# A decoder layer on one core: the place of the cross-attention's output product among the transposes of its step

## The chip, the cores and the metric

The kernel runs on one core of a Trainium2 chip. The metric is the device time of one execution, in microseconds (us). The kernel before took 2285.08 us, the median of three runs (2284.96 to 2286.03).

A core has five engines, each with an instruction queue of its own: TensorE (PE in the profile; its weight loads are shown apart, as PEld), VectorE (DVE), ScalarE (ACT), GpSimd (POOL) and SyncE (SP), which issues most of the transfers. Matrix products go into PSUM, which the kernel uses as eight banks of 128 x 512 floats; everything else lies in SBUF.

## What is computed

One decoder layer with the normalisation behind each block, for 32 sequences of 256 tokens and 256 features:

```
x = layernorm(x + self_attention(x))            # 16 query heads of 64, 4 key heads, rotary, alibi
x = layernorm(x + cross_attention(x, ctx, ctx)) # 16 heads of 16, windows of 64, rotary, mask by cell
x = layernorm(x + feed_forward(x))              # 8-bit activations, ternary weights, 1024 inner
```

The part that the change touches is the end of the cross-attention. Its heads' outputs `o` of one token are normalised, projected, and added to the residual; then the sum is normalised:

```
y = _ln(o, ln_o_w, ln_o_b) @ w_o.T + b_o
x = layernorm(x + y)
```

In the kernel the scale `ln_o_w` is multiplied into the weights beforehand, and bias terms are already in the residual.

## The kernel before

A batch is one sequence: two tiles of 128 tokens (t = 0 and 1). The program is written out as slots, two to a step (part 0 and part 1), eight steps to a batch. In every step one eighth of a batch's self-attention runs: transposes `t` of the last step's probabilities (`self_turn`, L447), scores `s` for this step (`self_scores`, L394), and in every second step the values `o` (L464) and the spread of the inverse sums `R` (L479). A second pipeline runs nine steps behind with the cross-attention: scores `xs` (L656), exponentials (L686), transposes `xt` (`cross_turn`, L695), values `xo` (`cross_values`, L711), and transposes back `xr` (`cross_back`, L731). Everything else is written as generators that do a piece of work at each slot: the projections of the next batch (`self_inputs`, L331), the self-attention's output (`self_output`, L495), the context's keys and values (`cross_inputs`), the cross-attention's output (`cross_output`) and the feed-forward (`feed_forward`, L798 and L845). A number that a generator yields is the number of slots until its next piece; nothing means one.

TensorE, VectorE and ScalarE run their instructions exactly in the order in which the program issues them (`manual_schedule`). The order on GpSimd and SyncE is set by the framework. So the order of the calls within a slot decides what waits behind what. In a slot the generators that are due run first. Then in part 0 come the self-attention's transposes, `cross_back` and `cross_turn`, then the deferred ScalarE scalings in `last` (`flush`), and then the scores. In part 1 come `cross_values` and the normalisation of the self-attention's output (`self_normal`, L487). What is left in `last` is issued at the end of each slot.

`cross_output(b, t)` starts 29 + 8t slots after its batch. Its pieces are:

- the statistics of the heads' output `on` (VectorE) and their reciprocal deviation `rstd` (three GpSimd instructions, `rstd_of`, L185 to L187);
- one slot on, the scaling of `on` on ScalarE, put into `last` (`scaled`, L199);
- one slot on, `transposed`: two transposes `zoT` on TensorE (L205) and a copy into `zT` on ScalarE (L206);
- one slot on, in part 0, the product `xw` = zT x weights (L757), the sum with the residual into `x2` (VectorE, L761), its statistics and its `rstd`;
- one slot on, the scaling of `x2` on ScalarE, put into `last`.

The product's slot is part 0 of a step: of step 16 after the batch's start for the first tile, of step 20 for the second. Generators come first, so on TensorE `xw` stands ahead of that step's transposes `t`, `xr` and `xt`. `feed_forward(b)` begins with the maximum of both tiles of `x2` (VectorE) in step 21.

In the names of the profile, `zT` is the transposed normalised output, `xw` the PSUM bank of the product, `xoT` the copy of the values that `xr` transposes, `pT` and `xpT` the copies of the transposed probabilities of the two attentions.

Of the kernel before, what the change touches and what calls it, by code (L numbers as in the profile page):

```python
# [13 lines left out]
ALU = mybir.AluOpType  # L14
# [5 lines left out]
D = 256  # L20
NDC = D // P
# [29 lines left out]
def kernel(  # L51
# [27 lines left out]
    nc = tc.nc  # L79
# [5 lines left out]
    def ctile(shape, dtype, name):  # L85
        return const.tile(shape, dtype, name=name, tag=name)
# [3 lines left out]
    def bank(name, shape=(P, 512), dtype=F32):  # L90
        return ps.tile(list(shape), dtype, tag="b", name=name)
# [12 lines left out]
    def work(name, shape, bufs=2, dtype=F32):  # L104
        return sb.tile(list(shape), dtype, tag=name, name=name, bufs=bufs)

    def small(name, n):
        return sb.tile([P, 8], F32, tag="small", name=name, bufs=48)[:, 0:n]
# [31 lines left out]
    xo_w = ctile([P, NDC, D], F32, "xo_w")  # L140
# [15 lines left out]
    for i in range(2):  # L156


        t = ctile([P, (NT + 1) * XH * XE + 32 - XE], F32, f"xvaug{i}")
# [14 lines left out]
    def stats(src, name):  # L174

        st = small("st", 6)
        mv = small(f"mv_{name}", 2)
        nc.vector.bn_stats(st, src)
        nc.vector.bn_aggr(mv, st)
        return mv  # L180

    def rstd_of(mv, name):

        rb = small(f"rstd_{name}", 2)
        nc.gpsimd.tensor_scalar(rb[:, 0:1], mv[:, 1:2], EPS, None, ALU.add)  # L185
        nc.gpsimd.tensor_tensor(rb[:, 0:1], rb[:, 0:1], neg_half[:, 0:1], ALU.pow)
        nc.gpsimd.tensor_scalar(rb[:, 1:2], mv[:, 0:1], rb[:, 0:1], -1.0, ALU.mult, ALU.mult)  # L187
        return rb


    last = []

    def flush():
        while last:
            last.pop(0)()
# [5 lines left out]
    def transposed(dst, src, name):  # L201

        pt = bank(name)
        for dc in range(NDC):
            nc.tensor.transpose(pt[:, dc * P : (dc + 1) * P], src[:, dc * P : (dc + 1) * P], ident)  # L205
        nc.scalar.copy(dst, pt[:, 0 : NDC * P].rearrange("p (c t) -> p c t", t=P))  # L206
# [537 lines left out]
    def cross_output(b, t):  # L744
        s = state[b]
        on = s["on", t]
        mv = stats(on, "zo")
        rstd = rstd_of(mv, "zo")
        yield
        last.append(partial(scaled, on, on, rstd))  # L750
        yield
        zoT = work("zT", [P, NDC, P])
        transposed(zoT, on, "zoT")
        yield
        py = bank("xw")
        for dc in range(NDC):
            nc.tensor.matmul(py[:, 0:D], zoT[:, dc, :], xo_w[:, dc, :], start=(dc == 0), stop=(dc == NDC - 1))  # L757
        if t == 0:
            s["x2"] = work("x2", [P, NT, D])
        h = s["x2"][:, t, :]  # L760
        nc.vector.tensor_tensor(h, py[:, 0:D], s["x1", t], ALU.add)  # L761
        mv = stats(h, "x2")
        rstd = rstd_of(mv, "x2")
        yield
        last.append(partial(scaled, h, h, rstd))


    def feed_forward(b):
# [102 lines left out]
    for b in range(B):  # L871
        s0 = 16 * b
        if b:
            at(s0 - 16, self_inputs(b))
        at(s0 + 2, cross_inputs(b))
        for t in range(NT):
            at(s0 + 2 * (5 + 4 * t), self_output(b, t))
            at(s0 + 2 * (CROSS + 5 + 4 * t) + 1, cross_output(b, t))
        at(s0 + 2 * (CROSS + 11) + 2, feed_forward(b))

    with tc.manual_schedule(engines={mybir.EngineType.PE, mybir.EngineType.DVE, mybir.EngineType.Activation}):
        running = []
        slot = min(starts)
        while starts or running:
            step, part = divmod(slot, 2)
            k, odd = divmod(step - CROSS, 2)
            for gen in starts.pop(slot, ()):
                running.append([slot, gen])

            def cross(f, unit, *more):  # L890
                if 0 <= unit < 4 * B:
                    f(*divmod(unit, 4), *more)

            def own(f, unit):
                if 0 <= unit < 8 * B:
                    f(*divmod(unit, 8))


            def pair(f):
                if step % 2 == 0 and 0 <= step // 2 - 1 < 4 * B:  # L900
                    f(*divmod(step // 2 - 1, 4))

            if part == 0:
                pair(self_inverse)
            else:
                pair(self_spread)
            if part == 1 and not odd:
                cross(cross_exp, k, 0)
            if part == 0 and odd:
                cross(cross_exp, k, 1)  # L910
            for r in list(running):
                if r[0] == slot:
                    wait = next(r[1], r)
                    if wait is r:
                        running.remove(r)
                    else:
                        r[0] += wait or 1
            if part == 0:
                own(self_turn, step - 1)
                if odd:  # L920
                    cross(cross_back, k - 1)
                    cross(cross_turn, k, 0)
                else:
                    cross(cross_turn, k - 1, 1)
                flush()
                own(self_scores, step)
                if not odd:
                    cross(cross_scores, k)
                pair(self_values)
            else:  # L930
                if not odd:
                    cross(cross_values, k - 1)
                pair(self_normal)
            flush()
            slot += 1

# [88 lines left out]
```

## Time and profile before

| | |
|---|---|
| median of 3 runs | 2285.08 us |
| profiled execution | 2288.16 us |
| its span, first to last instruction | 2286.3 us |
| mean granted TensorE clock | 0.985 |
| xw on TensorE (L757): records, mean | 256, 417 ns |
| copy into zT on ScalarE (L206): instances, median | 64, 358 ns |

The durations of the prediction come from the profiled execution. Its span is the time between its first and last instruction. A line of a list of waits names the engine and the line of the waiting instruction, then whom it waited for, and then the total in us, the number of times and the longest. The lines of a timeline have start and duration in us, the engine, the line, the operation, the output and the inputs, how many instructions are merged, and in brackets how long the engine was idle before and what ended it. `PEld` lines are weight loads. A product of 32-bit floats shows as two loads and two matmul records.

In the steady part of the run a batch takes 68.23 us: the first tile's product starts at 1101.92, 1170.16 and 1238.39 us, and the second tile's at 1134.79, 1203.02 and 1271.26.

### The profile page before, as it was taken

The numbers are of one execution on the slowest core, as the hardware profiler recorded it, in microseconds if no ns is written. First come the engines' busy times: TensorE is split into PE (matmuls) and PEld (weight loads), VectorE is DVE, ScalarE is ACT, GpSimd is POOL, SyncE is SP. The second block draws the span as 40 slices with busy tenths as digits, with TensorE's granted clock in tenths as the row PEclk, the third lists the DMA queues.
The fourth block names the chain that finished last, engine by engine and source line by source line (L and its number), as shares of the span: only waits on it lengthen the run. The fifth ranks groups of instructions, "written<-read, shape, count | busy, mean of one in ns | idle before, by whom it ended". The sixth has DMA issues, their size and how long they took to land.

```text
span 2286.3 us, 55642 instructions
## 1 busy us (share of the span) xinstructions
PE 2186.2 (96%) x17828; PEld 1653.7 (72%) x17828; DVE 1709.6 (75%) x6949; ACT 1692.1 (74%) x4961; POOL 1117.3 (49%) x1851
## 2 busy tenths in 40 slices
PE   7999999999999999999999999999999999999983
PEld 5677777777777777777777777777777777777651
DVE  3767777877777777777777777787777787777675
ACT  2677777878777878777878777778777777777762
POOL 5344555554555444545554545454545454545432
PEclk9999999999999999999999999999999999999986
DMA  6312222222222222222222222222222222222111
GB/s 215 89 52 55 65 67 59 58 58 59 66 66 59 59 58 63 64 64 60 60 58 67 57 64 63 60 57 68 55 65 62 62 54 68 59 57 56 31 31 31
DMA packets 191427, 144.09 MB, mean 63 GB/s; under 512 B 107808, under 2 KB 160928, under 8 KB 191136
## 3 DMA queue, kind: packets, MB, share of 16 engines
q1 hardware_dynamic: 189440, 136.95, 24.3%
q8 instruction: 144, 2.36, 0.4%
q10 hardware_dynamic: 1696, 3.57, 0.4%
q14 instruction: 147, 1.20, 0.2%
HBM read 39.50 MB, written 8.39 MB: 21 GB/s over the span
## 4 chain that ended last, share of the span: by engine, by line
PE 71%; DVE 12%; ACT 11%; DMA 2%; issue 2%; POOL 1%; SPq 0%; ACTq 0%; POOLq 0%; DVEq 0%
PE s L394 10%; PE proj L331 10%; PE wo L495 9%; PE t L447 8%; PE o L464 8%; ACT p L420 4%; DVE p L410 4%; PE xt L695 4%; DVE gu L813 3%; PE xw L757 3%; ACT xp L686 3%; PE xv L616 3%; PE ffo L845 2%; PE R L479 2%; PE xk L604 2%; PE v L363 2%
## 5 line engine op out<-in xcount | busy, mean ns | idle before, releaser
L420 ACT ACTIVATE p<-p,nm 128x256 f32<-128x256 f32 x1024 | 507.9, 498 | 156.1 <-DVE nm L410 152.3
L410 DVE CUSTOM_DVE_ANT_0 p<-s,alibi 128x256 f32<-128x256 f32 x1024 | 372.3, 420 | 167.8 <-PE s L394 167.8
L452 ACT COPY pT<-t 128x512 f32<-128x512 f32 x512 | 274.8, 590 | 190.7 <-PE t L447 190.1
L686 ACT ACTIVATE xp<-xp,xnm 128x128 f32<-128x128 f32 x1024 | 326.0, 394 | 4.3 <-DVE xnm L670 4.3
L394 PE MATMUL s<-kT,qT 64*128 64x256 f32 x2048 | 290.9, 403 | 0.0
L447 PE MATMUL t<-ident,p 128*128 128x128 f32 x2048 | 269.2, 274 | 3.2 <-ACT p L420 3.2
L447 PEld LDWEIGHTS t<-ident,p 128*128 128x128 f32 x2048 | 240.4, 141 | 34.8 <-ACT p L420 6.6
L464 PE MATMUL o<-pT,v 128*64 128x256 f32 x2048 | 249.3, 385 | 0.0
L331 PE MATMUL proj<-xT,wq_sb 128*128 128x256 f32 x1024 | 249.1, 387 | 0.0
L495 PE MATMUL wo<-wo_sb,oT 128*128 128x256 f32 x1024 | 245.3, 382 | 0.0
L355 POOL TENSOR_TENSOR qT<-qT,other 128x512 f32<-128x512 f32 x128 | 163.7, 1279 | 152.0 <-DMA other<-psin 83.7
L670 DVE CUSTOM_DVE_ANT_0 xp<-xs,mask 128x128 f32<-128x128 f32 x1024 | 225.7, 286 | 0.9 <-PE xs L656 0.9
L394 PEld LDWEIGHTS s<-kT,qT 64*128 64x128 f32 x2048 | 176.6, 186 | 54.7 <-issue 32.8
L495 PEld LDWEIGHTS wo<-wo_sb,oT 128*128 128x128 f32 x1024 | 189.4, 190 | 33.8 <-issue 10.6
L331 PEld LDWEIGHTS proj<-xT,wq_sb 128*128 128x128 f32 x1024 | 185.6, 191 | 32.7 <-DVE xnm L670 5.9
L464 PEld LDWEIGHTS o<-pT,v 128*64 128x64 f32 x2048 | 136.0, 136 | 97.4 <-issue 41.1
L420 ACT ACTIVATION_READ_ACCUMULATOR p<-p,nm 128x1 f32 x1024 | 192.4, 188 | 0.0
L340 DVE TENSOR_TENSOR psin<-proj,rs_sb 128x512 f32<-128x512 f32 x160 | 110.2, 689 | 96.7 <-PE proj L331 96.5
L697 ACT COPY xpT<-xt 128x512 f32<-128x512 f32 x256 | 153.6, 600 | 8.3 <-PE xt L695 6.6
L695 PE MATMUL xt<-ident,xp 128*128 128x128 f32 x1024 | 155.1, 275 | 0.0
L566 POOL TENSOR_TENSOR qb<-qb,rx_sb 128x256 f32<-128x256 f32 (+1 forms) x96 | 87.7, 913 | 128.9 <-ACT xp L686 76.6
L813 DVE SCALAR_TENSOR_TENSOR gu<-gu,ff 128x512 f32<-128x512 f32 x128 | 82.1, 681 | 74.6 <-ACT gu L812 74.6
(150 smaller groups left out, 4365.0 us busy)
## 6 DMA issues: line engine op xcount, KB each, us to landing
other<-psin SPq DMA_DIRECT2D x640, 64.0 KB, 2.0
xT<-in_xt_dram SPq DMA_DIRECT2D x32, 256.0 KB, 2.9
xs<-in_x_dram SPq DMA_DIRECT2D x32, 256.0 KB, 3.1
cs<-in_ctx_dram SPq DMA_DIRECT2D x32, 256.0 KB, 2.7
other<-qb SPq DMA_DIRECT2D x64, 128.0 KB, 2.0
kTz<-tr SPq DMA_DIRECT2D x256, 32.0 KB, 2.0
other<-qb SPq DMA_DIRECT2D x128, 64.0 KB, 1.9
out_dram<-x SPq DMA_DIRECT2D x32, 256.0 KB, 2.3
```

What stands on the lines that cost most here:

```text
L331: nc.tensor.matmul(pq[:, c * L : (c + 1) * L], w[:, dc, c * P : (c + 1) * P], xT[:, dc, :], start=(dc == 0), stop=(dc == NDC - 1),)
L355: nc.gpsimd.tensor_tensor(d2, d2, other, ALU.add)
L394: nc.tensor.matmul(banks[half][:, rr * L : (rr + 1) * L], qT[rows_, rr, qc * P : (qc + 1) * P], kT[rows_, kc, :], start=(rr == 0), stop=(r ...
L410: nc.vector.tensor_tensor_reduce(p[:, cols], banks[half][:, cols], alibi[:, 2 * (4 * kc + 2 * rp + rr) + half, :], -0.125, 3.0e38, ALU.add ...
L420: nc.scalar.activation(p[:, cols], p[:, cols], AF.Exp, bias=nm[:, rr : rr + 1], scale=-1.0, accum_out=s["sums", i // 2][:, (2 * rp + rr) * ...
L447: nc.tensor.transpose(pt[:, j * P : (j + 1) * P], p[half][:, rr * L + kk * P : rr * L + (kk + 1) * P], ident,)
L452: nc.scalar.copy(pT[half], pt)
L464: nc.tensor.matmul(po[half * HD : (half + 1) * HD, rp * L : (rp + 1) * L], s["v"][:, kk, (2 * kc + half) * HD : (2 * kc + half + 1) * HD], ...
L495: nc.tensor.matmul(py[:, 0:D], s["oT", qc, kc][:, r, :], wo_sb[:, 4 * kc + r, :], start=(kc == 0 and r == 0), stop=(kc == 1 and r == 3),)
L670: nc.vector.tensor_tensor_reduce(p[:, cols], banks[2 * half + j // 2][:, j % 2 * P : (j % 2 + 1) * P], s["mask"][:, qc, :], -1.0, 3.0e38, ...
L686: nc.scalar.activation(p[:, cols], p[:, cols], AF.Exp, bias=s["xnm", i][half][:, j : j + 1], scale=-1.0)
L695: nc.tensor.transpose(pt[:, j * P : (j + 1) * P], p[:, j * P : (j + 1) * P], ident)
```

## The change

The work of the product is put into a function and handed to a new list, `late`. The first tile's generator yields one slot more ahead of it. `late` is emptied at two places of a slot: in part 0 behind `cross_back` and `cross_turn` and ahead of `flush` and the scores, and in part 1 at the end, behind `self_normal`. So the first tile's product, its sum and its statistics are issued at the end of part 1 of step 16 instead of at the beginning of its part 0, and its `x2` is scaled in part 0 of step 17 instead of at the end of part 1 of step 16. The second tile's product is issued in the same slot as before, behind that step's transposes and ahead of its scores, and its `x2` is scaled in the same place as before.

```diff
+    late = []
...
         transposed(zoT, on, "zoT")
-        yield
-        py = bank("xw")
-        for dc in range(NDC):
-            nc.tensor.matmul(py[:, 0:D], zoT[:, dc, :], xo_w[:, dc, :], start=(dc == 0), stop=(dc == NDC - 1))
+        yield 1 + (t == 0)
         if t == 0:
             s["x2"] = work("x2", [P, NT, D])
         h = s["x2"][:, t, :]
-        nc.vector.tensor_tensor(h, py[:, 0:D], s["x1", t], ALU.add)
-        mv = stats(h, "x2")
-        rstd = rstd_of(mv, "x2")
-        yield
-        last.append(partial(scaled, h, h, rstd))
+        more = {}
+
+        def product():
+            py = bank("xw")
+            for dc in range(NDC):
+                nc.tensor.matmul(
+                    py[:, 0:D], zoT[:, dc, :], xo_w[:, dc, :], start=(dc == 0), stop=(dc == NDC - 1)
+                )
+            nc.vector.tensor_tensor(h, py[:, 0:D], s["x1", t], ALU.add)
+            mv = stats(h, "x2")
+            more["rstd"] = rstd_of(mv, "x2")
+
+        late.append(product)
+        yield
+        last.append(partial(scaled, h, h, more["rstd"]))
...
                 else:
                     cross(cross_turn, k - 1, 1)
+                while late:
+                    late.pop(0)()
                 flush()
                 own(self_scores, step)
...
                 pair(self_normal)
+                while late:
+                    late.pop(0)()
             flush()
```

The order of instructions that results, on each engine that it touches (before, then after):

```
first tile
  TensorE  xw t xr xt s o R wo                     t xr xt s o R xw wo
  VectorE  add+stats xrinv on p.. oT hib           xrinv on p.. oT add+stats hib
  ScalarE  oT x2 pT pT xpT p..                     oT pT pT xpT x2 p..
  GpSimd   rstd qb other xqT gu gu                 qb other xqT gu rstd gu
second tile
  TensorE  xw t xr xt s                            t xr xt xw s
  VectorE  add+stats xrinv on p..                  xrinv on add+stats p..
  ScalarE  as before
  GpSimd   as before
```

The order of SyncE's transfers is the same in both kernels.

## The prediction

> **What bounds the kernel now.** First the busy shares of the page, to see which engine can set the end:
>
> ```profile
> PE 2186.2 (96%) x17828; PEld 1653.7 (72%) x17828; DVE 1709.6 (75%) x6949; ACT 1692.1 (74%) x4961; POOL 1117.3 (49%) x1851
> ```
>
> TensorE is busy 96% of the span; no other engine passes 75%. So time can be won only where TensorE stands still, and the second view is the list of who waited for whom (total us, times, longest us):
>
> ```profile
> PE xw L757 <- ACT zT L206: 34.0, 63, 2.9
> PE ffo L845 <- DMA hiT<-hib: 16.6, 4, 9.1
> PE ff L798 <- DMA xiT<-xib: 9.4, 2, 8.4
> ...
> PEld xw L757 <- ACT zT L206: 61.6, 63, 3.2
> ...
> ACT pT L452 <- PE t L447: 190.1, 161, 3.3
> ```
>
> The output product xw is the only place where TensorE waits in every batch: 63 of its 64 instances. All its other waits come 1 to 10 times. ScalarE in turn waits 190.1 us for TensorE's transposes, so elsewhere it is TensorE that is waited for. Third, the chain of waits around batch 15 (start, us, what), to see how the wait sits in the path that sets the end:
>
> ```profile
> 1168.67 0.68 ACT xp L686 x2
> 1169.35 0.50 ACT qb L550 x2
> 1169.85 0.26 ACT zT L206
> 1170.12 0.04 issue
> 1170.16 1.13 PE xw L757 x4
> 1171.29 0.87 PE t L447 x8
> ```
>
> From this xw the chain stays on TensorE to the scores at 1197.32. Then it leaves for VectorE's and ScalarE's softmax, and it comes back through zT into the second tile's xw at 1203.02. So the zT copy, queued behind exponentials and the query bias on ScalarE, is what holds TensorE. Fourth, the timeline of weight loads and of ScalarE there; it has the distances I use (start, us, engine, line):
>
> ```profile
> 1168.39 0.55 PEld L798 LDWEIGHTS <-xiT 128*128 128x128 bf16 x4
> 1170.16 0.73 PEld L757 LDWEIGHTS xw<-xo_w,zT 128*128 128x128 f32 x4 [1.23 <-ACT zT L206]
> 1170.91 1.01 PEld L447 LDWEIGHTS t<-ident,p 128*128 128x128 f32 x8
> 1171.89 0.25 PEld L731 LDWEIGHTS xr<-ident,xoT 128*128 128x128 f32 x2
> ```
>
> ```profile
> 1169.76 0.35 ACT L206 COPY zT<-zoT 128x256 f32<-128x256 f32 x1
> 1170.01 0.37 ACT L720 COPY xoT<-xo 128x256 f32<-128x256 f32 x1
> 1170.27 1.28 ACT L686 ACTIVATE xp<-xp,xnm 128x128 f32<-128x128 f32 x4
> 1171.82 1.07 ACT L452 COPY pT<-t 128x512 f32<-128x512 f32 x2 [0.26 <-PE t L447]
> ```
>
> The picture repeats with the period of a batch (first tile's xw at 1170.16 and 1238.39, 68.23 us apart). In the timeline the load sits idle 1.23 us before nearly every first-tile product and 0.58 to 0.60 us before nearly every second-tile one. 31 and 29 instances have this pattern or a longer wait; the last batches differ.
>
> **The Trainium skill.** "TensorE: Matmul & The Clock Gate", section "Step-by-step: what each phase is for", says that matmuls stay in program order and only weight loads are pulled ahead. The trace agrees: zT is the operand that is loaded, the load itself waits (61.6 us), and nothing behind it runs. "PSUM — Partial Sum Buffer", section "Engine vs sequencer instructions", says that the queues of ScalarE, VectorE and GpSimd are strictly first in, first out; here zT goes at 1169.76, right after the bias at 1169.26, although its transposes were loaded at 1167.38. "Perfetto Trace Analysis", section "Identifying the Most-Contended Engine", warns that matmul busy time overstates TensorE. The load row, 72%, leaves more room, but the chain, 71% on TensorE, says that it is the bound all the same.
>
> **The change part by part.** No arithmetic, transfer or buffer is added or removed, and SP's queue keeps its order. Three moves per batch count.
>
> First tile. On TensorE xw leaves its place ahead of the eight transposes t and goes one slot on, behind R and ahead of wo. The group t can be loaded 0.76 us after the feed-forward load (same pair at 1161.61 and 1162.37), at 1169.15; xr 0.98 us later (1170.91 to 1171.89), at 1170.13. But xr loads xoT, the copy right behind zT, which ends at 1170.38; a load follows its copy by 0.05 (zT ended 1170.11, load 1170.16), so xr goes at 1170.43, after a new wait of 0.30. It went at 1171.89: 1.46 us sooner. Later xw costs its four passes; eight such passes of wo take 1.62 (1176.08 to 1177.70), so 0.81. Net 0.65 us.
>
> Second tile. xw goes behind t, xr, xt and ahead of the scores s. The projection loaded at 1200.84 takes 1.62, t follows at 1202.46, xr at 1203.44 (xoT ended 1203.24: no wait), xt 0.21 later, xw 0.47 after that at 1204.12, s 0.81 + 0.17 later at 1205.10. It was loaded at 1205.61: 0.51 us sooner. Then o, 1.06 after s, at 1206.16. Its fourth matmul, about 0.56 in (6 of 16 loads that take 1.49), needs the second pT copy, which ended at 1206.85, and ScalarE cannot be sooner: it works without a gap from 1196.54. So up to 0.18 of the 0.51 is lost again. I take 0.42, between 0.33 and 0.51.
>
> VectorE moves with it: add, statistics and aggregate, 0.42 + 0.43 + 0.18, about 1.0 us. For the first tile they land behind the oT product and ahead of hib of the feed-forward, where VectorE had idled 0.54 for GpSimd's gu; hib has 5 us of slack, as its transposed copy lands 3.1 us after an issue at 1184.80 and is used at 1193.14. For the second tile they stand ahead of the score reductions; the add can start at 1205.3, VectorE is free again at about 1206.4, and the scores are there 1.17 us after their load (1205.61 to 1206.78), at 1206.27. That costs 0.1 us at most, hidden because ScalarE is busy until 1207.31. Without that cover it would be 0.1 x 29 = 3 us.
>
> ScalarE and GpSimd. The first tile's scaling of x2 (0.60 us) now stands in the next step, between the xpT copy and the exponentials, and waits there for GpSimd's rstd, whose three operations (0.23 + 0.57 + 0.27, about 1.25 with gaps) stand after the first of two gu operations of 1.12. VectorE's statistics end at about 1177.5, gu at about 1178.1, so rstd is done at about 1179.4 and xpT at about 1179.5: no wait. ScalarE there had 1.36 us idle ahead of the exponentials. Second tile: its rstd stays behind the same rotations (begun at 1207.68), its scaling stays at 1210.28.
>
> Sum: 31 x 0.65 + 29 x 0.42 = 20.2 + 12.2 = 32.4 us. The profiled execution took 2288.16 us (span 2286.3); less 32.4 that is 2255.8. The median of the runs is 3.1 lower, 2285.08, so I expect 2253.
>
> **The rivals.** More is won: neither xr nor o waits, because ScalarE runs a little ahead of the trace. For it: both remainders, 0.30 and 0.18, are small. Against: ScalarE's queue has no gap there. 31 x 0.95 + 29 x 0.51 = 44.2, that is 2241.
>
> Less is won: at the second tile the wait only moves, to o (for pT) or to xk (for zcT, whose copies ended 0.6 us ahead of the load at 1211.00), and the first tile keeps half. For it: the unbroken ScalarE queue from 1196.54 to 1210.9. Against: the margins worked out above. 31 x 0.33 = 10, that is 2275.
>
> Slower: ScalarE stands in the first tile's x2 scaling. If GpSimd gets to rstd only behind the second gu, which ended at 1182.20, rstd is done at 1183.5; the exponentials start at 1184.1 instead of 1181.53, and the next xoT copy, which ended at 1185.04 with its load at 1186.13, comes 2.6 later: TensorE loses 2.6 - 1.1 = 1.5 us in a batch. 31 x 1.5 = 46 against 32 won: 2299. It decides once rstd ends later than about 1181.9. Against it: in the order of instructions rstd stands ahead of the second gu, and its inputs (1177.5) are there 4 us before that point. The waits show ScalarE stopped by rstd_x only 5.6 us in all.
>
> No change: zT's wait is replaced in full by xoT's and pT's, 2285. The distances speak against it.
>
> **How the numbers follow.** Forecast 0.64 (2244 to 2264: first tile 0.5 to 0.8, second 0.2 to 0.51), more 0.14, less 0.13, no change 0.03, slower 0.06. The range 2239 to 2273 takes in most of "more" and the nearer part of "less". A difference below 0.2% cannot be told from none in this kernel. Faster 0.91, same 0.03, slower 0.06.
>
> **What would show it.** In the profile after, the wait of xw for zT is gone at both tiles. A wait of xr for xoT of about 0.3 us stands at the first tile only, and perhaps one of o for pT at the second. The distance from one batch's first xw to the next is about 67.2 us. If instead ScalarE's L199 waits for rstd_x in every batch, or TensorE waits for p at t, the rival that ends slower is at work. A distance of 66.8 means that xr did not wait.

## The result, and the profile after

The changed kernel took 2258.61 us, the median of four runs (2256.52 to 2261.18), beside 2285.43 for four runs of the kernel before: a ratio of 0.9883, with a 95% interval of 0.9866 to 0.9900. It is 27 us faster; 32 were expected. The profiled execution took 2257.97 us, with a span of 2256.0.

First the page of the changed kernel: the busy shares, and the chain that ended last by engine.

```profile
PE 2188.3 (97%) x17828; PEld 1660.7 (74%) x17828; DVE 1708.6 (76%) x6949; ACT 1680.8 (75%) x4961; POOL 1126.7 (50%) x1851
...
PE 89%; DVE 4%; ACT 3%; DMA 2%; POOL 1%; issue 1%; SPq 0%; POOLq 0%; ACTq 0%; DVEq 0%
```

The last line of the kernel before, from its page:

```profile
PE 71%; DVE 12%; ACT 11%; DMA 2%; issue 2%; POOL 1%; SPq 0%; ACTq 0%; POOLq 0%; DVEq 0%
```

TensorE now makes up 89% of the chain, where it was 71%; VectorE and ScalarE together fell from 23% to 7%. The same work is done in less time. Next the list of who waited for whom, of TensorE and of its weight loads (total us, times, longest us):

```profile
PE xr L734 <- ACT xoT L723: 12.0, 6, 4.4
...
PE xw L766 <- ACT zT L209: 0.5, 1, 0.5
...
PE o L467 <- ACT pT L455: 0.2, 1, 0.2
...
PEld t L450 <- ACT qb L553: 8.4, 30, 0.3
```

The product's wait for zT is gone: 0.5 us once, where it was 34.0 in 63 places. The wait of xr for xoT that was expected in every batch is not there; its six entries lie at the edges of the run. In its place, 30 times, the transposes t wait for qb. The timeline of weight loads at a first tile (start, us, engine, line; the idle time ahead in brackets) shows where:

```profile
1222.14 0.55 PEld L808 LDWEIGHTS <-xiT 128*128 128x128 bf16 x4
1222.80 0.57 PEld L450 LDWEIGHTS t<-ident,p 128*128 128x128 f32 x4
1223.66 0.42 PEld L450 LDWEIGHTS t<-ident,p 128*128 128x128 f32 x4 [0.29 <-ACT qb L553]
1224.18 0.20 PEld L734 LDWEIGHTS xr<-ident,xoT 128*128 128x128 f32 x2
1224.35 0.47 PEld L698 LDWEIGHTS xt<-ident,xp 128*128 128x128 f32 x4
```

and ScalarE at the same place:

```profile
1223.01 0.60 ACT L553 ACTIVATE qb<-xq,xbcol 128x128 f32<-128x128 f32 x2
1223.50 0.36 ACT L209 COPY zT<-zoT 128x256 f32<-128x256 f32 x1
1223.76 0.38 ACT L723 COPY xoT<-xo 128x256 f32<-128x256 f32 x1
```

The second four transposes of t load 0.05 us after qb has ended (1223.61). They do not read qb: they write a PSUM bank. In the program as built, xq, which qb reads, and these four transposes lie in the same bank in each of the 30 batches in which the wait stands. So the bank is free once qb has read it. xr follows at 1224.18, 0.04 after the copy xoT has ended (1224.14); behind the transposes alone it could have gone at about 1224.05, as the run below with xoT copied first shows. So two things hold this place, the bank and, 0.13 us longer, xoT.

The timeline of weight loads at a second tile of the changed kernel:

```profile
1188.20 1.01 PEld L450 LDWEIGHTS t<-ident,p 128*128 128x128 f32 x8
1189.18 0.26 PEld L734 LDWEIGHTS xr<-ident,xoT 128*128 128x128 f32 x2
1189.40 0.47 PEld L698 LDWEIGHTS xt<-ident,xp 128*128 128x128 f32 x4
1189.83 0.73 PEld L766 LDWEIGHTS xw<-xo_w,zT 128*128 128x128 f32 x4
1190.90 0.73 PEld L397 LDWEIGHTS s<-kT,qT 64*128 64x128 f32 x8 [0.33 <-issue]
1191.96 1.73 PEld L467 LDWEIGHTS o<-pT,v 128*64 128x64 f32 x16 [0.33 <-issue]
1194.08 0.42 PEld L482 LDWEIGHTS R<-ident,wide 128*128 128x128 f32 x4 [0.39 <-issue]
```

and the last three of these groups in the kernel before:

```profile
1205.61 0.73 PEld L394 LDWEIGHTS s<-kT,qT 64*128 64x128 f32 x8 [0.17 <-issue]
1206.67 1.49 PEld L464 LDWEIGHTS o<-pT,v 128*64 128x64 f32 x16 [0.33 <-issue]
1208.55 0.42 PEld L479 LDWEIGHTS R<-ident,wide 128*128 128x128 f32 x4 [0.38 <-DVE nm L410]
```

Here nothing waits by name, but two distances have grown: xw to s is 1.07 us, with an idle of 0.33 where 0.17 stood ahead of s before, and o to R is 2.12, where it was 1.88.

Because a batch repeats to a few hundredths of a microsecond, the distance from one first-tile product to that of the next batch is a finer measure than the time. It was 68.23 us and is 67.35 (each the median over the steady batches, all within 0.02): 0.88 us less, and thirty times that is 26.4 us. It comes from one profiled execution of each kernel; in both, the granted clock was 1.00 from 100 to 2150 us and lower only at the ends. The table gives all that changed in it by more than 0.02 us, from the distances between weight loads (changed kernel minus kernel before):

| | first tile | second tile |
|---|---|---|
| group ahead of the product's old place (wait for zT gone) | -1.11 | -0.56 |
| t to xr | +0.40 | 0 |
| xr to xt | -0.05 | 0 |
| xt to the next group | 0 | -0.21 |
| xw to the next group | 0 | +0.31 |
| wo behind xw instead of R | +0.10 | |
| o | 0 | +0.24 |
| sum | -0.66 | -0.22 |

### The profile page after: what moved, and what is told of

Read it like the earlier page. It is cut to its first block, busy times and chain, and to the rows that moved or that the text cites. A ratio compares the mean times of both kernels' runs of the same rounds, so it can differ in the third digit from the quotient of the medians.

```text
span 2256.0 us, 55618 instructions
## 1 busy us (share of the span) xinstructions
PE 2188.3 (97%) x17828; PEld 1660.7 (74%) x17828; DVE 1708.6 (76%) x6949; ACT 1680.8 (75%) x4961; POOL 1126.7 (50%) x1851
## 4 chain that ended last, share of the span: by engine, by line
PE 89%; DVE 4%; ACT 3%; DMA 2%; POOL 1%; issue 1%; SPq 0%; POOLq 0%; ACTq 0%; DVEq 0%
PE proj L334 13%; PE s L397 11%; PE o L467 10%; PE wo L498 10%; PE t L450 9%; PE xt L698 5%; PE ff L808 4%; PE xs L659 3%; PE R L482 3%; PE xo L714 3%; PE xv L619 3%; PE ffo L855 2%; PE xq L535 2%; PE xw L766 2%; PE xk L607 2%; PE v L366 2%
## 5 line engine op out<-in xcount | busy, mean ns | idle before, releaser
L450 PE MATMUL t<-ident,p 128*128 128x128 f32 x2048 | 275.2, 274 | 3.8 <-ACT p L423 2.5
L467 PE MATMUL o<-pT,v 128*64 128x256 f32 x2048 | 257.0, 386 | 0.2 <-ACT pT L455 0.2
L467 PEld LDWEIGHTS o<-pT,v 128*64 128x64 f32 x2048 | 142.2, 136 | 99.0 <-issue 32.0
```

Source lines behind the costliest of these rows:

```text
L450: nc.tensor.transpose(pt[:, j * P : (j + 1) * P], p[half][:, rr * L + kk * P : rr * L + (kk + 1) * P], ident,)
L467: nc.tensor.matmul(po[half * HD : (half + 1) * HD, rp * L : (rp + 1) * L], s["v"][:, kk, (2 * kc + half) * HD : (2 * kc + half + 1) * HD], ...
```

## The experiments

Every one starts from the changed kernel and computes the same. The kernel before was run beside them. Its median was 2286.85 us beside four of them (each tile alone, xoT ahead of zT, the context's scaling later) and 2285.97 beside the other four. The columns of the summary are the median, the ratio to the kernel before with its interval, and the distance from batch to batch, which is that of the profiled execution.

| run | median us | ratio | us a batch |
|---|---|---|---|
| before | | | 68.23 |
| changed | 2258.61 | 0.9883 (0.9866 to 0.9900) | 67.35 |
| first tile alone | 2265.23 | 0.9906 (0.9890 to 0.9923) | 67.57 |
| second tile alone | 2279.70 | 0.9968 (0.9957 to 0.9980) | 68.00 |
| first tile in its own slot | 2263.18 | 0.9889 (0.9871 to 0.9906) | 67.35 |
| xoT ahead of zT | 2256.54 | 0.9867 (0.9852 to 0.9881) | 67.27 |
| context's scaling later | 2250.98 | 0.9844 (0.9829 to 0.9858) | 67.12 |
| products ahead of xr | 2258.12 | 0.9875 (0.9857 to 0.9892) | 67.28 |
| exponentials later | 2254.16 | 0.9855 (0.9840 to 0.9870) | 67.18 |
| all three | 2244.61 | 0.9811 (0.9795 to 0.9827) | 66.77 |

**Do the two moves add up?** One part of the change at a time.

```diff
-        late.append(product)
+        if t == 0:
+            late.append(product)
+        else:
+            product()
```

> Only the first tile's product is moved (a slot later); the second tile's stays at the head of its step. If the two moves add up and the first is worth 1.11 (wait gone) - 0.40 (t and xr wait) - 0.10 (wo behind a product) + 0.05 = 0.66 us in a batch, as the distances of weight loads in the changed kernel say: 31 x 0.66 = 20, 2265 us, and 67.6 us from batch to batch. If the gain came mostly from the second tile: 2275 or more. The wait of xw for zT is left at the second tile alone, about 0.6 us each.

Measured: 2265.23 us and 67.57 from batch to batch, 0.66 less than before. The wait of xw for zT is left 32 times in the list, at the second tile.

The other way round (`t == 1`, and the plain `yield`):

> Only the second tile's product is moved behind its step's transposes; the first tile's stays. If it is worth what the distances in the changed kernel say (0.56 wait gone, 0.21 + 0.02 between xt and s, less 0.31 before s and 0.24 within o: about 0.22 us in a batch): 29 x 0.22 = 6, 2279 us, 68.0 us from batch to batch. If it is worth the 0.42 of the prediction: 12, 2273 us.

Measured: 2279.70 us and 68.00, that is 0.23 less. 0.66 and 0.23 make 0.89, and both moves together gave 0.88: they add up, and three quarters of the gain come from the first tile.

**Is it the later slot?** The first tile's product is handed over in its old slot, so it stands behind that step's transposes, like the second's.

```diff
-        yield 1 + (t == 0)
+        yield
```

> As the changed kernel, but the first tile's product also stays in its step, behind the transposes and ahead of the scores, like the second tile's. If the first tile's gain comes from standing behind the transposes alone, the slot itself is worth nothing: the 0.10 us at wo is saved, and about 0.10 is paid between xw and s. 2258 us, within 3. If the slot later is what gives the gain: 2265 or more.

Measured: 67.35 from batch to batch, the same as the changed kernel to a hundredth, and a span of 2256.2 beside 2256.0. The median, 2263.18, lies above the 2258 expected by more than the 3 us allowed. These runs scattered from 2258.02 to 2263.4, as the kernel before beside them did (2285.27 to 2292.22). The scatter goes with the mean granted clock: it was 0.986 in the run of 2258.02, which is the profiled one, and 0.983 in the other three; for the kernel before it was 0.985 in the fastest run and 0.981 in the slowest. In the profiled run the clock was 1.00 from 100 to 2150 us. So by the batch, the slot is worth nothing; leaving the place ahead of the transposes is what counts. By the times alone 5 us stay open. ScalarE's scaling of x2 stands in its old place here, and with it ScalarE's waits for GpSimd's rstd of x2 fall from 20.1 us in 25 places to 7.9 us in 6 (5.6 in 4 in the kernel before). As the batch is no shorter, those waits cost nothing.

**What holds the first tile's t and xr?** The copy of zT is taken out of `transposed` and put into `late`, so that xoT is copied first.

```diff
-        transposed(zoT, on, "zoT")
+        pt = bank("zoT")
+        for dc in range(NDC):
+            nc.tensor.transpose(pt[:, dc * P : (dc + 1) * P], on[:, dc * P : (dc + 1) * P], ident)
+        late.append(partial(nc.scalar.copy, zoT, ...))
```

> As the changed kernel, but ScalarE copies xoT ahead of zT, so xoT comes 0.26 us sooner and zT 0.26 later. If the first tile's t and xr stand 0.40 us longer because xr waits for xoT: 0.26 won in a batch, 31 x 0.26 = 8, 2250 us. If they stand because the second four transposes of t need the PSUM bank that the query projection held until ScalarE's qb (it ends at 1223.61, the transposes load at 1223.66): nothing, 2258 us, and xr still 1.38 us after t.

Measured: 2256.54 us and 67.27, 0.08 less than the changed kernel instead of 0.26. The timeline of weight loads of this run:

```profile
1222.09 0.57 PEld L450 LDWEIGHTS t<-ident,p 128*128 128x128 f32 x4
1222.95 0.42 PEld L450 LDWEIGHTS t<-ident,p 128*128 128x128 f32 x4 [0.28 <-ACT qb L553]
1223.34 0.25 PEld L734 LDWEIGHTS xr<-ident,xoT 128*128 128x128 f32 x2
```

The wait for the bank is still there, 0.28 us. Only the distance from the second four transposes to xr shrank, from 0.52 to 0.39. So neither branch of the expectation was right: xoT holds xr last, by 0.13 us, and right behind it stands the bank, which alone keeps 0.27 of the 0.40. Of the 0.13, 0.05 is lost again from xr to xt (0.22 instead of 0.17). The other way to test it is to bring qb itself forward: the exponentials of the cross-attention's first half move from the beginning of the slot, where they stand even ahead of the generators, to behind `cross_values`.

```diff
-            if part == 1 and not odd:
-                cross(cross_exp, k, 0)
...
                     cross(cross_values, k - 1)
+                    cross(cross_exp, k, 0)
```

> As the changed kernel, but the four exponentials of the cross-attention's first half (1.2 us) are issued behind the copy of xoT instead of ahead of qb, so qb, zT and xoT come 1.2 us sooner. If the bank held for qb and the copy of xoT are all that holds the first tile's t and xr: both waits (0.40) go, and xt then waits about 0.2 for the exponentials; 0.2 a batch, 31 x 0.2 = 6, 2252 us, and t to xr back to 0.98 us. If a third thing holds them: 2258. If the later exponentials hold other steps: slower than 2258.

Measured: 2254.16 us and 67.18, 0.17 less. t to xr is back to 0.98 us, as the timeline of its weight loads shows, and xt doesn't wait either:

```profile
1219.38 1.01 PEld L450 LDWEIGHTS t<-ident,p 128*128 128x128 f32 x8
1220.36 0.25 PEld L734 LDWEIGHTS xr<-ident,xoT 128*128 128x128 f32 x2
1220.58 0.47 PEld L698 LDWEIGHTS xt<-ident,xp 128*128 128x128 f32 x4
```

So the bank and xoT are all that held it. Less was won than the 0.40 because 0.05 is lost again from xr to xt, and because o now takes 2.04 to 2.06 us there instead of 1.88: TensorE is sooner at o than ScalarE at its copies. The records of o's single matmuls at this place show the copy pT behind it: up to there they start in pairs, and one whose partner starts at 1222.77 starts at 1222.90 instead, 0.05 us after the second copy of pT has ended (1222.85).

**What lengthens the second tile's o?** ScalarE gets 1.0 us of other work out of the way of pT: the scaling of the context is issued one slot later.

```diff
-        yield
+        yield 2
         zc = cs
...
-        yield 2
+        yield
         zcT = work("tr", [P, NDC, L], 3)
```

> As the changed kernel, but the scaling of the context (two ScalarE instructions, 1.0 us together) is issued half a step later, behind the copies of pT and xpT in the second tile's step. If o's matmuls stand 0.24 us there because they wait for pT: o back to 1.88 us from 2.12, 29 x 0.24 = 7, 2252 us. If o is longer for another reason: 2258 us. If the exponentials behind it come late: slower than 2258.

Measured: 2250.98 us and 67.12, 0.23 less. The timeline of weight loads of this run:

```profile
1187.20 0.73 PEld L397 LDWEIGHTS s<-kT,qT 64*128 64x128 f32 x8 [0.33 <-issue]
1188.27 1.49 PEld L467 LDWEIGHTS o<-pT,v 128*64 128x64 f32 x16 [0.33 <-ACT pT L455]
1190.14 0.42 PEld L482 LDWEIGHTS R<-ident,wide 128*128 128x128 f32 x4 [0.38 <-DVE nm L413]
```

o to R is 1.87 us again. So o had waited for pT, though the list of waits of the changed kernel has that only once, for 0.2 us. Its single matmul records say the same: one that would have started with its partner at 1192.45 starts at 1192.64, 0.05 after the second copy of pT has ended (1192.59). Behind it the pairs no longer start together, and the last starts 1.81 us after the first, where it was 1.56 in the kernel before. The wider idle ahead of s, 0.33, stays.

**Another place for the product.** Both products between t and xr of their own step:

```diff
-        yield 1 + (t == 0)
+        yield
...
                 own(self_turn, step - 1)
+                while late:
+                    late.pop(0)()
```

(and not behind `cross_turn`).

> As the changed kernel, but both products stand between the transposes t and xr of their own step. The first tile's t still waits for the bank that qb frees (about 0.29), but xr comes a product later and no longer waits for xoT, and wo follows R again: about 0.13 us a batch won. At the second tile the wider gap ahead of s (0.33 after a product, 0.17 after transposes) is saved, and o's wait for pT grows by as much: nothing. 31 x 0.13 = 4, 2254 us. If neither mattered: 2258.

Measured: 2258.12 us and 67.28, 0.07 less than the changed kernel; in the time, no difference can be told. The first tile's t waits 0.28 us for the bank, xr no longer waits, and ahead of s the idle is back to 0.17. But xr to xt now takes 0.32 or 0.33 instead of 0.22: the 0.10 that wo paid behind the product is paid there.

**The remainders together.** Three of the edits at once: the products ahead of xr, the exponentials behind xoT, the context's scaling later.

> The products between t and xr, the exponentials behind xoT, and the context's scaling half a step later, all together. If the three remainders are independent: the first tile gains 1.1 and the second 0.5 us a batch against the kernel before, 31 x 1.1 + 29 x 0.5 = 49, 2237 us, 66.6 us from batch to batch. If ScalarE becomes the bound once TensorE runs without a wait: 2245 to 2251.

Measured: 2244.61 us (2241.72 to 2246.0), a ratio of 0.9811, and 66.77 from batch to batch. The timeline of weight loads at a first tile of this run:

```profile
1213.86 0.54 PEld L808 LDWEIGHTS <-xiT 128*128 128x128 bf16 x4
1214.52 1.01 PEld L450 LDWEIGHTS t<-ident,p 128*128 128x128 f32 x8
1215.50 0.73 PEld L766 LDWEIGHTS xw<-xo_w,zT 128*128 128x128 f32 x4
1216.26 0.36 PEld L734 LDWEIGHTS xr<-ident,xoT 128*128 128x128 f32 x2
```

No wait is left there: the feed-forward's loads to t are 0.66 us, t to the product 0.98. Against the kernel before the batch gains 1.10 and 0.56 and pays 0.10 or 0.11 at each xr, 1.46 in all, which is the measured 68.23 - 66.77. It is faster than both kernels. 2237 had been expected, from 1.6 us a batch; 30 x 0.14 = 4 us of the difference come from those gaps behind the product, and the rest is no more than the runs scatter. The time alone would fit the other branch, that ScalarE becomes the bound (2245 to 2251); the batch does not: no group of TensorE's loads takes over 0.02 us longer than in the kernel before, except xr.

## Why the prediction was right, point by point

What bounds the kernel: right. With the wait for zT gone the time fell by 27 us, and the chain lies on TensorE for 89% instead of 71%.

The first tile, 0.65 us: 0.66 measured, by the change and by its part alone. The step behind it held: xr was to go when xoT has been copied, and it does, 0.04 us after. What the prediction did not have is a second hold, which ends 0.13 us earlier: the second half of t waits 0.28 or 0.29 us for a PSUM bank. The two end nearly together, since ScalarE does qb, zT and xoT in a row. So the bank changed nothing in the sum, by the trace; taking the bank alone away was not tried. The prediction noted that no buffer is added and did not ask when the bank of t comes free. It had been shared before too: in the kernel before as built, xq and the first four of these transposes lie in one bank in every steady batch. There the product stood ahead of them and waited for zT, which ScalarE copies behind qb, so the bank's wait was covered.

That the sum is right to 0.01 is in part luck. The 0.10 that wo takes longer behind a product was missed, and it was set off by 0.05 less for the product's own loads (0.76, not 0.81) and 0.05 less from xr to xt.

The second tile, 0.42 us: 0.22 to 0.23 measured. This is the term that was mis-sized, and it accounts for the 5.6 us between 2253 and 2258.61 (29 x 0.2 = 6). Two parts of it failed. The idle ahead of s was put at 0.17, as it stands behind transposes; behind the product it is 0.33. Shorter distances ahead of it (xt to xw 0.44 instead of 0.47, the product's loads 0.74 instead of 0.81) took most of that back, so that s came 0.46 us sooner instead of 0.51. And o's wait for pT was put at 0.09, half of its bound of 0.18; o takes 0.24 longer. The one matmul is held for 0.19, close to the bound; the rest is lost because its pairs fall out of step. The mechanism, that part of the gain is lost again to the unbroken queue of ScalarE, was right.

VectorE's move cost nothing, as argued: no group of TensorE grew beyond those of the table. ScalarE's scaling of x2 in the next step was to go without a wait; in most of the steady batches it waits for rstd, for up to 0.95 us. That hurt nothing, by the run with the first tile in its own slot: the idle time ahead of the exponentials, 1.36 before, covers it. The rival that ends slower needed rstd more than 2 us later than reckoned, and that did not happen.

More won, less won and no change: the result lies between the forecast and "less won", inside the forecast's own range of 2244 to 2264. Its case, that the wait only moves to o, came true in part at the second tile.

## What to carry to other kernels

Where an engine that bounds the kernel runs in order, put an instruction that needs a fresh result of another engine behind work whose inputs are long there; the same step's transposes were enough, and a whole slot more gave nothing. Then measure what the followers wait for, because the next result in the other engine's queue is only a copy's length behind: here nearly half of the 1.67 us that TensorE no longer waited for zT in a batch was lost, most of it to a bank, a copy and a queue. Moving other work of ScalarE out of the way, and the products ahead of xr, raised the gain from 0.88 to 1.46. When a wait is taken away, ask of what stood behind it not only when its inputs are ready but also who reads last from the buffer that it writes: the wait for the bank had been there all along, covered by the one for zT.

## What had not been expected of the hardware

A wait inside a group of matmuls can leave next to nothing in the list of waits: o took 2.12 us instead of 1.88 because of pT, while o's waits for pT add up to 0.2 us in the whole run. The distance between the first loads of two groups shows it. And holding one of o's paired matmuls for 0.19 us made the group end 0.24 later.

What stood ahead of a group changed its times: the idle ahead of the scores s was 0.16 or 0.17 us behind transposes and 0.33 behind a product of 32-bit floats. And two groups took 0.10 us longer behind the product: wo 1.72 instead of 1.62 behind R, and xr to xt 0.32 instead of 0.22 behind t. It isn't so for all: t to xr is 0.98 us behind the product in the kernel before, and 0.98 behind the feed-forward's loads in the run with the exponentials later.
